# Seven products instead of eight in the first mix and the values, with VectorE's work handed out differently

## The chip, the cores and the metric

The kernel runs on one core of a Trainium2 chip. The metric is the device time in microseconds of one execution. Before the change the median of three runs is 464.14 us (464.13 to 464.68). All data is float32.

## The reference, cut to what matters

The input X has 4 batches of 1024 tokens with 256 features. Four blocks follow each other, and each adds its result to x:

```python
x = x + attn(layernorm(x))      # causal attention, one head of 256
x = x + ffn(layernorm(x))       # "first mix"
x = x + state(layernorm(x))     # gated state-space block
x = x + ffn(layernorm(x))       # "second mix", the same weights

# attn: Q, K, V = X Wq' + bq, X Wk' + bk, X Wv' + bv
#       out = softmax(causal(Q K' / 16)) V
# ffn:  xr, xk = mixtures of x and x one token earlier (mu_r, mu_k)
#       out = sigmoid(xr W_r') * (relu(xk W_k')^2 W_v')
# state: x_proj, z = split(xn W_in' + b_in); a long convolution over 16 states;
#       out = ((conv W_C' + D x_proj) * silu(z)) W_out' + b_out + xn
```

## The kernel before

A batch of 1024 tokens is two halves of 512; a half is numbered j from 0 to 7, and a tile of 128 tokens i from 0 to 31. A matrix of 256 features lies as two chunks of 128 partitions. Nearly all the work of TensorE is dense float32 products, and each shows in the trace as two records with a weight load each.

The program does not write out the order of the engines' work. Python code describes units of TensorE work (`o.unit`) and operations of the other engines (`o.op`), each with what it needs, an estimated cost and the engines that could do it ("ways"). A planner (`class Order`) plays this through with its own model of time, tries twenty sets of its parameters, and emits the instructions of the plan that ends first. Units come in the order in which the code lists them, and the planner may take any of the next nine (`AHEAD`). An operation with two ways goes to the engine that would end it first. A way written `DVE+port`, and every way of `POOL`, also takes a port that the two share in the planner's model. Sums with memory operands alone can go to VectorE or GpSimd, copies out of PSUM to ScalarE or VectorE.

PSUM is two pairs of banks (`pair`, for scores of up to 1024 columns) and four single banks (`bank`, for everything else). In SBUF, 34 slots of equal size hold all the tiles that come and go.

The stages, in order of time:

- *Attention*, from 15 to 253 us: a loop over the 32 tiles. For each: scores (`scores`, L1550), their minimum and exponents, a transpose by way of DRAM, and the weighted sum with the values (`weigh`, L1655). The queries of a half come from `queries` (batches 0 and 1) or from `queries_of_batch` (2 and 3). Values come tile by tile from `values` (L1522): two products of 257 columns, whose last column is a bias for the scores, and an addition of the bias row on VectorE (L1532).
- *First mix* (`mix1`): from i = 10 on, one half in four tiles is worked on beside the attention: keys (`keys`, two units of two products of 512 columns, then relu and square), gates (`gates`, products of 256 columns, then tanh), values (`values`, then a product with the gate on VectorE, L1095, and an addition to x on GpSimd, L1101). Halves 5, 6 and 7 end behind the loop, up to 278 us. `state_prepare` follows each half's values: layer norm and transpose for the state block.
- *State block*, 278 to 397 us: gates and skips of batch 0 plain, of batches 1 to 3 by seven products, the convolution, and outputs of each half (`outputs(j)`), behind which the second mix of that half is prepared.
- *Second mix* (`mix2`), up to the end: keys of batches 0 to 2 by seven products, all gates and values plain. The layer-norm sums of halves 0 to 5 are done on ScalarE (`BY_SCALAR = 6`), the others by VectorE's statistics.

*Seven products.* Where a 256 by 256 weight matrix meets a batch's 256 by 1024 data, both are seen as two by two blocks, and eight block products of 512 columns can be had with seven. `stream_sums` makes four sums of data blocks (T1 to T4, on GpSimd or VectorE, L832), `weight_sums` four of weight blocks, once. `seven_products` is a chain: product 1 goes into the first half of a PSUM pair (the chain) and is copied out (u1); product 2 has a bank of its own and gives the first result; product 6 is accumulated onto product 1 in place, copied out (u2); product 5 goes to the second half; product 7 onto the chain, copied out (u3); product 4 onto the chain, which is the second result; product 3 onto product 5. Three of the four results are sums of a PSUM part and a copy, made by VectorE (L905, L907). A chain yields after each product, and the caller mixes its steps with other units (`go_on`, `next(chain)`, `more_gates`, `advance`).

Of the kernel before, what the change touches and what calls it, by code (L numbers as in the profile page):

```python
# [19 lines left out]
P = 128  # L20
# [10 lines left out]
SLOT = 4 * (D + 1)  # L31
# [10 lines left out]
BY_SCALAR = 6  # L42
# [11 lines left out]
class Order:  # L54
# [17 lines left out]
    SURE = 0.5  # L72
    FRONT = 12.0
# [182 lines left out]
    def _way(self, time, n):  # L256

        if self.log[n]["moves"]:
            time = max(time, self.queue - self.FLIGHT - 0.5)
        return min(  # L260
            (self._start(time, w) + w[1], self._start(time, w), w[0], w[2])
            for w in self.log[n]["ways"]
        )
# [96 lines left out]
def dve(n):  # L360
    return 0.02 + n / 850
# [7 lines left out]
def hybrid_kernel(  # L369
# [41 lines left out]
    slots = ctx.enter_context(tc.tile_pool(name="slots", bufs=34))  # L411
# [92 lines left out]
    wv = new("wv", KC, D + 1)  # L504
    bv_r = new("bv_r", D + 1)
    bq_c, bk_c, dsk, dt_c = (new(n, KC) for n in ("bq_c", "bk_c", "dsk", "dt_c"))
# [14 lines left out]
    load(2.0, "wv", *stream_rows(wv[:, :, :D], WvT), *per_row(bv_r[:, :D], bv))  # L521
# [62 lines left out]
    def normalized(  # L584
# [36 lines left out]
        def stats(n):  # L621
            nc.vector.bn_stats(st()[:, n, :], row(n))  # L622
            nc.vector.bn_aggr(mv()[:, n, :], st()[:, n, :])
# [77 lines left out]
        else:  # L701
            for n in range(NH):
                o.op(f"{key}.st{n}", [needs[n]], ("DVE", 0.53, partial(stats, n)))
            variances_of, shifts_of = variances, shifts
        for n0, n1 in spans:
            span = "" if n1 - n0 == NH else f"{n0}"
            some = range(n0, n1)
            o.op(
                f"{key}.ve{span}", [f"{key}.st{n}" for n in some],
# [105 lines left out]
    def stream_sums(key, src, needs):  # L815
# [9 lines left out]
        for k, plus, minus in (  # L825
# [5 lines left out]
            def emit(engine, k=k, plus=plus, minus=minus):  # L831
# [4 lines left out]
                ("POOL", 1.05, partial(emit, nc.gpsimd)), ("DVE+port", dve(HALF), partial(emit, nc.vector)),  # L836
# [3 lines left out]
    def seven_products(key, sums_key, a, s_of, src, t_of, add_to, direct, needs, there):  # L840


        u = lazy(lambda: slot(f"u_{key}"))
        held = lazy(lambda: pair(f"held_{key}"))

        def part(k):
            return lambda: u()[:, ts(k, HALF)]

        def chain():
            return held()[:, :HALF]  # L850

        def shared():
            return held()[:, HALF:]

        def unit(r, w, data, need, dst, takes=None, first=True):
            o.unit(
                f"{key}.p{r}", columns(HALF), needs + need,
                lambda: nc.tensor.matmul(  # L858
                    dst(), lhsT=w(), rhs=data(), start=first, stop=True, skip_group_check=True
                ),  # L860
                takes,
            )

        def kept(name, r, k, more=()):
            o.op(f"{key}.{name}", [f"{key}.p{r}", *more], *copies(part(k), chain))

        unit(1, lambda: a(0, 0), lambda: src(0)[:, 0, :], there, chain, "pair")
        kept("u1", 1, 0)
        yield
        p = lazy(lambda: bank(f"p2_{key}"))  # L870
        unit(2, lambda: a(0, 1), lambda: src(0)[:, 1, :], there, p, "bank")
        o.op(
            f"{key}.c11", [f"{key}.p2", f"{key}.u1"],
            ("DVE", dve(HALF) + 0.03, partial(add_to, 0, 0, p, part(0))), frees="bank",
        )
        yield
        unit(6, lambda: s_of(2), lambda: t_of(2), [f"{key}.u1", f"{sums_key}.T2"], chain, first=False)
        kept("u2", 6, 1)
        yield
        unit(5, lambda: s_of(1), lambda: t_of(1), [f"{key}.p1", f"{sums_key}.T1"], shared)  # L880
        yield
        unit(7, lambda: s_of(3), lambda: t_of(3), [f"{key}.u2", f"{sums_key}.T3"], chain, first=False)
        kept("u3", 7, 0, [f"{key}.c11"])
        o.op(
            f"{key}.c22", [f"{key}.p5", f"{key}.u3"],
            ("DVE", dve(HALF) + 0.03, partial(add_to, 1, 1, shared, part(0))),
        )
# [1377 lines left out]
```

## Time and profile before

The profiled execution took 464.18 us; its span from the first to the last instruction is 462.4 us, and the granted clock of TensorE is 1.00 throughout.

| stretch (us) | what it holds | TensorE busy | VectorE busy | ScalarE busy | GpSimd busy |
|---|---|---|---|---|---|
| 0 to 80.9 | loads, first tiles of attention | 79.5 | 62.4 | 28.4 | 11.2 |
| 80.9 to 268 | attention and first mix | 187.1 | 166.1 | 90.2 | 52.1 |
| 268 to 346.8 | end of first mix, convolution, first outputs | 77.9 | 46.7 | 39.6 | 34.0 |
| 346.8 to 416.2 | outputs and second mix | 69.4 | 65.9 | 50.4 | 26.8 |
| 416.2 to 462.4 | end of second mix | 40.6 | 29.4 | 18.4 | 15.4 |

Busy time of TensorE is from the start of a record to its modelled end; records overlap, so a stretch is full when they also start one right behind the other. The chain of waits is followed back from the last instruction; a line of it names the engine and line that the end hung on. In the tables of operations the columns are line, engine, operation, output and inputs, sizes, count, busy us, mean ns of one, and the idle time before them with what ended it.

### The profile page before, as it was taken

What the parts mean: (1) busy time and instruction counts of PE and PEld (TensorE: products, weight loads), DVE (VectorE), ACT (ScalarE), POOL (GpSimd) and SP (SyncE); (2) the same over time, 40 slices, a digit from 0 to 9 for tenths busy, and PEclk for the clock granted to TensorE, in tenths of its full rate; (3) what the DMA queues carried; (4) which work ended last, traced back from release to release, by engine and by line L of the source; (5) the groups of instructions that cost most, each with busy time, mean ns of one, the idle gap of its engine ahead of it and who ended that gap; (6) DMA issues with size and microseconds to landing.
All of it is one profiled execution on the core that took longest, in us unless ns stands there. A gap on an engine that the chain in (4) does not pass through costs nothing.

```text
span 462.4 us, 6630 instructions
## 1 busy us (share of the span) xinstructions
PE 454.6 (98%) x2052; PEld 311.4 (67%) x2052; DVE 370.7 (80%) x914; ACT 227.0 (49%) x473; POOL 139.4 (30%) x145
## 2 busy tenths in 40 slices
PE   8999999999999999999999999999999999999996
PEld 5665776667786767776678774473565857686675
DVE  4898697989989888788989977425689989998852
ACT  3322334453284453554335755523467887743452
POOL 3001002303032412332221568512255216336240
PEclk9999999999999999999999999999999999999999
DMA  8067958684358641428784869503014042604522
GB/s 236 27 170 209 272 143 236 169 252 151 101 160 213 184 138 51 137 87 256 226 261 128 276 220 276 213 15 90 13 63 121 0 143 86 215 14 135 178 75 68
DMA packets 84915, 69.44 MB, mean 150 GB/s; under 512 B 20160, under 2 KB 82576, under 8 KB 84880
## 3 DMA queue, kind: packets, MB, share of 16 engines
q1 hardware_dynamic: 84064, 68.76, 50.2%
q8 instruction: 16, 0.26, 0.2%
q10 hardware_dynamic: 816, 0.26, 0.2%
q14 instruction: 19, 0.16, 0.1%
HBM read 40.54 MB, written 28.45 MB: 149 GB/s over the span
## 4 chain that ended last, share of the span: by engine, by line
PE 84%; DVE 10%; POOL 3%; issue 1%; SPq 1%; DMA 1%; ACT 0%; DVEq 0%; POOLq 0%
PE po L1655 14%; PE sc L1550 13%; PE pv L1522 6%; PE held_zs L858 3%; PE held_ss L858 3%; PE held_qs L858 2%; PE held_gks L858 2%; PE pc L1862 2%; PE dust L1339 1%; DVE T_gks L832 1%; DVE xr_g L977 1%; DVE xk_g L977 1%; POOL x L1101 1%; PE pp_a0.pq L793 1%; PE pp_g6.pk L793 1%
## 5 line engine op out<-in xcount | busy, mean ns | idle before, releaser
L1655 PE MATMUL po<-v,prT 128*128 128x256 f32 x288 | 67.6, 380 | 0.0
L1550 PE MATMUL sc<-xa,q 128*128 128x512 f32 (+3 forms) x192 | 66.9, 486 | 0.0
L1655 PEld LDWEIGHTS po<-v,prT 128*128 128x128 f32 x288 | 54.2, 189 | 11.6 <-issue 3.1
L1571 ACT ACTIVATE pr<-pr,nmx 128x128 f32<-128x128 f32 (+7 forms) x32 | 24.7, 773 | 69.7 <-DVE pr L1566 57.1
L1550 PEld LDWEIGHTS sc<-xa,q 128*128 128x128 f32 x192 | 34.8, 190 | 24.3 <-issue 20.1
L1522 PE MATMUL pv<-wv,xa 128*128 128x257 f32 x128 | 32.7, 380 | 0.0
L1101 POOL TENSOR_TENSOR x<-x,r_f 128x512 f32<-128x512 f32 x16 | 20.8, 1298 | 35.7 <-DVE r_f L1095 33.8
L1522 PEld LDWEIGHTS pv<-wv,xa 128*128 128x128 f32 x128 | 23.9, 191 | 8.4 <-issue 4.1
L1608 DVE STREAM_TRANSPOSE prT<-pblocks 128x384 f32<-128x384 f32 (+7 forms) x30 | 24.0, 798 | 4.8 <-DMA pblocks<-exps 4.8
L661 POOL TENSOR_TENSOR rs_h<-ve_h,minus_half 128x8 f32<-128x8 f32 x8 | 13.2, 1646 | 47.9 <-DVE ve_h L650 47.9
L1566 DVE TENSOR_SCALAR_CACHE_REDUCE pr<-sc,v 128x128 f32<-128x128 f32 (+7 forms) x32 | 26.2, 818 | 1.1
L661 POOL TENSOR_TENSOR rs_a<-ve_a,minus_half 128x4 f32<-128x4 f32 x7 | 7.4, 1060 | 62.8 <-DVE ve_a L648 52.9
L1101 POOL TENSOR_TENSOR x<-x,r_g 128x512 f32<-128x512 f32 x14 | 20.1, 1446 | 16.8 <-DVE r_g L1095 16.8
L1699 POOL TENSOR_TENSOR x<-x,bout_r 128x512 f32<-128x512 f32 x16 | 20.7, 1302 | 13.3 <-ACT x L1692 9.8
L1692 ACT ACTIVATE x<-x,mrs_h,rs 128x256 f32<-128x256 f32 x32 | 17.2, 588 | 6.5 <-DVE rs L1703 6.5
L1965 POOL TENSOR_TENSOR z<-z,skip 128x512 f32<-128x512 f32 x11 | 15.0, 1384 | 17.4 <-DVE skip L1961 17.3
L661 POOL TENSOR_TENSOR rs_f<-ve_f,minus_half 128x4 f32<-128x4 f32 x8 | 8.1, 1016 | 39.2 <-DVE ve_f L648 34.1
L1664 DVE SCALAR_TENSOR_TENSOR x<-po,rsm,x 128x256 f32<-128x256 f32 x32 | 14.9, 467 | 5.4 <-PE po L1655 5.3
L622 DVE BATCH_NORM_STATS2 st_a<-x 128x6 f32<-128x256 f32 x32 | 13.0, 407 | 3.0 <-DMA x<-in_L_attn_a_X_dram 3.0
L974 ACT ACTIVATE xk_g<-hT_g,muk 128x512 f32<-128x512 f32 x16 | 11.0, 713 | 8.4 <-DVE hT_g L750 8.4
L1532 DVE TENSOR_TENSOR v<-pv,bv_r 128x257 f32<-128x257 f32 x32 | 13.2, 413 | 2.2 <-PE pv L1522 1.8
L977 DVE SCALAR_TENSOR_TENSOR xr_g<-hT_g,mur,xr_g 128x512 f32<-128x512 f32 x16 | 14.4, 920 | 0.5 <-ACT xr_g L974 0.5
(478 smaller groups left out, 1070.3 us busy)
## 6 DMA issues: line engine op xcount, KB each, us to landing
hk<-r_dram SPq DMA_DIRECT2D x16, 512.0 KB, 6.6
rows_g<-xn_g SPq DMA_DIRECT2D x8, 512.0 KB, 3.0
blocks_g<-rows_g SPq DMA_DIRECT2D x32, 128.0 KB, 2.7
x<-in_L_attn_a_X_dram SPq DMA_DIRECT2D x7, 512.0 KB, 5.1
rows_f<-xn_f SPq DMA_DIRECT2D x7, 512.0 KB, 3.5
blocks_f<-rows_f SPq DMA_DIRECT2D x28, 128.0 KB, 2.7
rows_h<-xn_h SPq DMA_DIRECT2D x7, 512.0 KB, 3.3
blocks_h<-rows_h SPq DMA_DIRECT2D x28, 128.0 KB, 2.9
```

What stands on the lines that cost most here:

```text
L661: nc.gpsimd.tensor_tensor(rs()[:, :k].rearrange("p k n -> p (k n)"), ve()[:, :k].rearrange("p k n -> p (k n)"), minus_half[:, : k * NH], A ...
L858: lambda: nc.tensor.matmul(dst(), lhsT=w(), rhs=data(), start=first, stop=True, skip_group_check=True),
L977: nc.vector.scalar_tensor_tensor(t()[:, c, :], hT()[:, c, :HALF], mu1[:, c : c + 1], t()[:, c, :], ALU.mult, ALU.add,)
L1101: nc.gpsimd.tensor_add(xg, xg, r()[:, ts(g, 2), :])
L1522: nc.tensor.matmul(pv()[:, : D + 1], lhsT=xaj()[:, c, ts(n, P)], rhs=wv[:, c, :], start=(c == 0), stop=(c == KC - 1),)
L1550: nc.tensor.matmul(sc()[:, k * HALF : k * HALF + w], lhsT=qh()[:, c, ts(n, P)], rhs=keys[k]()[:, c, :w], start=(c == 0), stop=(c == KC - 1),)
L1566: nc.vector.tensor_scalar(dst, src, v[2 * b + h]()[:, n, D : D + 1], None, ALU.add, ALU.min, accum_out=nmx(),)
L1571: nc.scalar.activation(p()[:, :nk], p()[:, :nk], AF.Exp, bias=nmx(), scale=-1.0, accum_out=sm())
L1608: nc.vector.transpose(dst()[:, : NH * width].rearrange("p (k m a) -> p k m a", m=NH, a=GRP), blocks().rearrange("p m (k a) -> p k m a", a= ...
L1655: nc.tensor.matmul(po()[:, :D], lhsT=src()[:, ts(n, P)], rhs=v[2 * b + n // NH]()[:, n % NH, :D], start=(n == 0), stop=(n == t),)
L1692: nc.scalar.activation(xt, xt, AF.Identity, bias=mrs()[:, 0, n : n + 1], scale=rs1()[:, n : n + 1])
L1699: nc.gpsimd.tensor_add(xg, xg, bout_r.unsqueeze(1).to_broadcast([P, 2, D]))
```

## The change

- Keys and gates of batches 0 to 2 in the first mix are made by seven products per batch (`keys_of_batch`, and a new `gates_of_batch` with products of 128 columns, the data block as the weights). The two chains are stepped in turn (`mixed`), from the sixth tile of the next batch on.
- Values of batches 2 and 3 of the attention are made by seven products per half of the tiles (`values_of_batch`, products of 129 columns), stepped in turn with the queries' chain (`attended`), whose data sums they share. The row of values has 258 columns, a zero column first.
- These chains, the queries' too, take two single banks instead of a pair.
- The bias of the values is no longer added to the values but to x, by GpSimd (`shifted`, in `attend_prepare`); the values leave PSUM by a copy. The column for the scores still gets its bias, by GpSimd, one tile at a time (`whole_bias`).
- The planner counts 0.5 us more for a way of VectorE where there is another (`SPARED`), after 24 us. Stream sums and the gated product on GpSimd are estimated at 1.25 us instead of 1.05. The aggregations of layer-norm statistics become one operation behind the four statistics.
- Second mix: `BY_SCALAR` is 3 instead of 6. Slots: 33 instead of 34.
- Values and state preparation of halves 4 and 5 stand behind the loop, after keys and gates of half 6. In the last phase the state gates, outputs and keys are listed in another order.

```diff
-BY_SCALAR = 6
+BY_SCALAR = 3
...
+    SPARED = 0.5
...
+        for engine, cost, emit in ways:
+            start = self._start(time, (engine, cost, emit))
+            late = start + cost
+            if len(ways) > 1 and engine[:3] == "DVE" and time > 2 * self.FRONT:
+                late += self.SPARED
+            if late < best:
+                best, chosen = late, (start + cost, start, engine, emit)
...
-    slots = ctx.enter_context(tc.tile_pool(name="slots", bufs=34))
+    slots = ctx.enter_context(tc.tile_pool(name="slots", bufs=33))
...
+    def row_products(tiles, width, *of):
+
+        def emit(dst, w, data, first):
+            for n, t in enumerate(tiles):
+                nc.tensor.matmul(
+                    dst()[:, ts(n, width)], lhsT=data()[:, ts(t, P)], rhs=w(),
+                    start=first and n == 0, stop=True, skip_group_check=True,
+                )
+
+        return len(tiles) * width, columns(width, len(tiles)), operands(*of), emit
...
         u = lazy(lambda: slot(f"u_{key}"))
-        held = lazy(lambda: pair(f"held_{key}"))
+        if kind == "pair":
+            held = lazy(lambda: pair(f"held_{key}"))
+            chain, shared = lambda: held()[:, :n], lambda: held()[:, HALF : HALF + n]
+        else:
+            banks = [lazy(lambda k=k: bank(f"held{k}_{key}")) for k in range(2)]
+            chain, shared = lambda: banks[0]()[:, :n], lambda: banks[1]()[:, :n]
...
+        def gates_of_batch(self, b, kind):
...
+            def add_to(e, h, p, u):
+                nc.vector.tensor_add(out(e, h), by_tile(p), by_tile(u))
...
+            T = stream_sums(key, src, there)
...
+        def shifted(g):
+            xg = x[b][:, h * NH + 2 * g : h * NH + 2 * g + 2, :]
+            nc.gpsimd.tensor_add(xg, xg, bv_r[:, :D].unsqueeze(1).to_broadcast([P, 2, D]))
...
-            ("DVE", dve(D), lambda: nc.vector.tensor_add(t()[:, n, :], pv()[:, : D + 1], bv_r)),
-            frees="bank",
+            *copies(lambda: t()[:, n, :], lambda: pv()[:, :VW], VW), frees="bank",
...
+            ("POOL", 0.15, lambda: nc.gpsimd.tensor_add(
+                t()[:, n, D + 1 :], t()[:, n, D + 1 :], bv_r[:, D:])),
...
+    def values_of_batch(b, T):
...
+        for g in range(2):
...
+            yield from seven_products(
+                key, f"qs{b}",
+                row_products(
+                    range(2 * g, 2 * g + 2), VW // 2, wv_block, lambda k: v_sums[:, k - 1, :], src, T
+                ),
+                add_to, direct, ["v_sums"], there, kind="bank",
+            )
...
+    def mixed(b):
+
+        keys, gates = mix1.keys_of_batch(b, "bank"), mix1.gates_of_batch(b, "bank")
+        for _ in range(7):
+            next(keys)
+            yield
+            next(gates)
+            yield
...
+    def attended(b):
+
+        queries = queries_of_batch(b)
+        next(queries)
+        yield
+        values = values_of_batch(b, query_sums[b])
+        for _ in range(6):
+            next(queries)
+            yield
+            next(values)
+            yield
+        for _ in values:
+            yield
...
+        if i % NT == 0 and SEVEN_FROM <= i // NT + 1 < NB:
+            chain = chain_of(partial(iter, chain), partial(attended, i // NT + 1))
+        if i % NT == 5 and 13 <= i:
+            chain = chain_of(partial(iter, chain), partial(mixed, i // NT - 1))
...
-    both(mix1.values, 5)
-    state_prepare(5)
-    more_gates(0)
-    mix1.keys(6, 0)
+    for unit in (
+        partial(mix1.keys, 6, 0), partial(mix1.keys, 6, 1),
+        partial(mix1.gates, 6, 0), partial(mix1.gates, 6, 1),
+    ):
+        next(chain, None)
+        next(chain, None)
+        unit()
+    for _ in chain:
+        pass
     mix1.transpose(7)
-    mix1.keys(6, 1)
-    both(mix1.gates, 6)
-    more_gates(0)
+    for j in (4, 5):
+        both(mix1.values, j)
+        state_prepare(j)
...
-    more_gates(5)
+    more_gates(2)
     mix_states(1)
+    more_gates(2)
     outputs(1)
-    more_gates(4)
+    more_gates(1)
     outputs(2)
-    more_gates(4)
+    more_gates(2)
+    outputs(3)
+    more_gates(2)
     mix_states(2)
```

## The prediction

> **What bounds the kernel now.** I read the page's busy shares and its chain first, then the table by stage, then the chain in order of time and the waits of TensorE, and last the rows of single operations.
>
> ```profile
> PE 454.6 (98%) x2052; PEld 311.4 (67%) x2052; DVE 370.7 (80%) x914; ACT 227.0 (49%) x473; POOL 139.4 (30%) x145
> ...
> PE 84%; DVE 10%; POOL 3%; issue 1%; SPq 1%; DMA 1%; ACT 0%; DVEq 0%; POOLq 0%
> ```
>
> A busy PE need not be a PE at its peak, so the starts of single products have to show it. The timeline at 110 us does:
>
> ```profile
> 108.67 2.33 PE L1655 MATMUL po<-v,prT 128*128 128x256 f32 x10
> 110.84 0.61 PE L1550 MATMUL sc<-xa,q 128*128 128x128 f32 x4
> 111.28 1.03 PE L1522 MATMUL pv<-wv,xa 128*128 128x257 f32 x4
> ```
>
> Ten records of 256 columns take 2.17 us to the next group's start, 0.217 each, and four of 128 columns take 0.44, 0.111 each (0.108 would be half of the 256). The pieces of the chain agree:
>
> ```profile
> 69.21 3.43 PE pp_a3.pq L793 x8
> ...
> 72.64 0.87 PE pv L1522 x4
> ...
> 89.02 1.73 PE pr_f0.pr L928 x8
> ```
>
> Eight records of 512 columns are 3.43 us, so one product (two records) is 0.858. Products stand back to back like this through the attention. What TensorE waits for in the whole span is little:
>
> ```profile
> PE pr_g4.pv L928 <- ACT ka_g L1047: 0.9, 1, 0.9
> PE held_gks L858 <- DVE u_gks L784: 0.9, 1, 0.9
> PE held_zs L858 <- DVE z L907: 0.6, 1, 0.6
> ```
>
> So each product left out is time won, as long as the other engines keep up. Who is near its limit is read by stage (columns: PE, PEld, DVE, ACT, POOL busy):
>
> ```profile
> 80.90:268.00 187.10, 187.10 (x807) 135.30 (x806) 166.14 (x444) 90.24 (x170) 52.08 (x51) 1.00 0.61 177
> 268.00:346.80 78.80, 77.92 (x504) 44.14 (x503) 46.73 (x93) 39.56 (x89) 33.99 (x31) 1.00 0.38 120
> 346.80:416.20 69.40, 69.40 (x278) 49.68 (x277) 65.94 (x112) 50.43 (x126) 26.76 (x27) 1.00 0.31 96
> ```
>
> The granted clock is 1.00. In the loop of attention and first mix (80.9 to 268) VectorE is 89% busy and TensorE never starves. From 346.8 to 416.2 VectorE is 95% busy and TensorE still runs full, so 95% is the most that this trace shows VectorE carrying without a loss.
>
> **TensorE, part by part.** *Keys* (three batches): eight products of 512 columns become seven; 3 x 0.858 = 2.6 us less. *Gates* (three batches): now 32 products of 256 columns per batch, four row pieces of 1.73 = 6.92 us. Then 7 x 4 products of 128 columns, each with its own weight load: 56 records at 0.111 = 6.22. Gain 0.7 each, 2.1 in all. *Values* (two batches): now eight tiles of 0.87 = 6.96. Then 2 x 7 x 2 products of 129 columns, 56 records at 0.111 = 6.22; gain 0.74 each, 1.5 in all. The sixteen tiles left alone grow from 257 to 258 columns, under 0.1. Sum: **6.1 us less on TensorE**, at 0.108 a record 6.7.
>
> Each seven-product run is a chain: product 6 waits for a copy out of PSUM, 7 and 4 for the next copies. Eleven such chains run today (two of queries, three each of gates, skips and second-mix keys), and the waits above charge two of them with 0.9 and 0.6: 0.14 a chain. The change adds ten (three keys, three gates, four values): **1.4 us back**. Ends: nothing, if other units always fill in, and 0.9 each, 9 us in all, if none does (first rival below).
>
> **VectorE.** Rows used:
>
> ```profile
> L1532 DVE TENSOR_TENSOR v<-pv,bv_r 128x257 f32<-128x257 f32 x32 | 13.2, 413 | 2.2 <-PE pv L1522 1.8
> ...
> L905 DVE TENSOR_TENSOR ka_g<-held_gks,u_gks 128x512 f32<-128x512 f32 x6 | 4.0, 674 | 1.4 <-ACT ka_g L1046 1.3
> L1038 DVE SCALAR_TENSOR_TENSOR ka_g<-ka_g 128x512 f32<-128x512 f32 x6 | 4.1, 676 | 0.1
> L1699 POOL TENSOR_TENSOR x<-x,bout_r 128x512 f32<-128x512 f32 x16 | 20.7, 1302 | 13.3 <-ACT x L1692 9.8
> L832 DVE TENSOR_TENSOR T_qs<-xa,T_qs 128x512 f32<-128x512 f32 x3 | 3.1, 1042 | 0.0
> ```
>
> Gone: 32 bias additions to v (13.2; the copies in their place fit on ScalarE) and three relus of 0.67 (2.0). New: 18 sums of 512 columns for keys and gates at 0.674 (12.1), 12 value sums at 0.413 (5.0), nine squarings at 0.676 (6.1; ScalarE could take them at 1.25), eight small weight sums at most 0.287 (the 128-column mask addition), 2.3. Net +10.3 with nothing moved. The half-microsecond handicap on VectorE moves work that has a second way: in the loop 16 normalized rows (8.5), six stream sums (5.2), seven more rows (2.7), two copies (1.4): up to 17.8. Net between -7.5 and +10.3; I take 0, most of two thirds moved, since ScalarE (90 of 187 us) has room for rows at 0.59 and six copies and two tanh in the new form.
>
> GpSimd takes 24 stream sums at 1.27 (30.5), sixteen bias additions to x at 1.30 (20.8) and 32 one-column additions at some 0.2 (a two-column copy took 0.19): about 58 us more, most of it in the loop, where it has 52. It is then at most 60% busy, but it works against VectorE: the stream sum on VectorE is 0.68 in its quiet form and 1.04 in the form of the row above, and the mixing sums xk_f and xr_f mean 0.81 and 0.77 in the loop against 0.68. That excess, 14 x 0.13 + 14 x 0.09 = 3.1 us, came with 52 us of GpSimd; twice the GpSimd adds 3 us to VectorE.
> The Trainium skill (SBUF — State Buffer, section "SBUF: two separate sides") says the port pair of the two engines is locked for a whole instruction and the other fully blocks. Estimated by that rule, 45 more GpSimd operations of 1.29 us, each meeting a two-input VectorE operation with chance 0.3 (some 45 of these in 187 us) and holding it for half its length, would cost 8.5 us, which speaks against the change.
> I keep the 3 of the rows.
>
> So VectorE has 166 + 0 + 3 = 169 of 181 us, 93%: under the 95% seen, and I charge nothing. If it gets +10.3 + 3 it has 179.5, which at 95% needs 189 us, 1.9 more than now.
>
> **Queues.** The transposes by DRAM of halves 4 to 7 are asked for four steps earlier, and values of halves 4 and 5 of the mix move behind the loop, with their state preparation (1 write, 4 reads each on SP) past two sets of keys and gates. SP issues the same transfers; DMA is 61% busy in the loop. The bias addition to x stands before the attention's own addition; GpSimd runs it tens of microseconds ahead of need, and late it would hold that addition's bank, then the next value product. The earlier halves hold their slots some 30 us longer (four tiles of the 32 that take 15 to 253 us), and there is one slot fewer (33): that costs nothing unless a T or u tile must wait for a slot; no row shows a slot wait, so 0 to 2 us, I take 0.
>
> **Last phase.** Statistics of three halves go back from ScalarE to VectorE: 12 x (0.41 + 0.18) = 7.1 us more, against up to 4.7 (rows), 5 (sums) and 4 (squarings) that the handicap moves away. The small aggregations of the statistics (0.18 each) are gathered behind the four statistics, as many as before. The finer order spreads state gates between outputs. Waits to be won there are the three above, 2.4 us; at the other end VectorE at 95% gives as much again. I take 0.5 won.
>
> **Sum.** -6.1 + 1.4 - 0.5 = -5.2. The profiled execution took 464.18 us (span 462.4 and 1.8 around it), as good as the median of 464.14: **459.0 us**. No change can be told within 0.2%, 0.9 us.
>
> **Rivals.** *Banks.* Two interleaved chains hold four single banks, all that there are, from the second one's fifth product to the first one's fourth. Until then no po, pv or gate product can start, only scores. Against: scores have their own pairs again, which queries took before. Seven such pairings, up to 2 x 0.65 of copies each, cost at most 9 us; half, 4.6, gives 464.18 - 6.6 + 4.6 = 462.2. Chance 0.17, ending between 461 and 465.
>
> *Slower: VectorE or the port becomes the bound in the loop.* Point: above 187.1 x 0.95 = 177.7 us of VectorE work, 11.6 more than now, the loop is longer than today. +10.3 and 3 for the port gives 189 in the loop and, other things equal, 466; with the 28 mixing sums each 0.36 longer, as the T_qs row is, the port costs 10.1 instead of 3.1 now, 7 more: 183.4 at 95% is 193, 470. For it: 18 new PSUM sums cannot leave VectorE, slices of today's loop stand at 11.37 of 11.58. Against: the 17.8 us that can move. Chance 0.22.
>
> *Pile-up behind the loop.* Four state preparations instead of three lie close: from values 4 to values 7 TensorE has 5 x 3.45 = 17.3 us, GpSimd needs 4 x (2 x 1.27 + 1.65 + 2 x 1.29) = 27. Urgent of it is 17, so it just fits; if the last half's statistics queue behind two additions of x, TensorE idles 2.6 to 5 us: 461.6 to 464. Chance 0.1.
>
> **Chances and range.** Forecast 0.51 (456 to 461.5, faster). Of banks, 0.10 is faster, 0.05 no change, 0.02 slower; of the pile-up, 0.05 is faster and 0.05 no change; VectorE's 0.22 is slower. Faster 0.66, same 0.10, slower 0.24. The range runs from 455.5 (0.108 a record, no chain waits, 2.4 won late: 464.2 - 6.7 - 2.4 = 455.1, rounded in) to 467.5, leaving out the dear end of VectorE.
>
> **What would show it.** Right: PE busy about 6 us less in all, gates and value products 0.111 apart, the loop under 183 us with TensorE still at 100% in it; VectorE's busy time within 5 us of 371, GpSimd's near 195. Wrong: rows of PE waiting for u_fks, u_frs, u_vs copies or VectorE sums above 0.2 us a chain; VectorE over 95% across the loop; a gap of TensorE before the last half's transposes (h7).

## The result and the profile after

The change takes **467.82 us** (median of 6 runs, 466.16 to 468.73) beside 464.55 us of the kernel before on the same chip (6 runs, 464.13 to 465.43): ratio of the means 1.0065, between 1.0044 and 1.0085 at 95%. It is slower by 0.65%, where 1.1% faster was forecast, and 467.82 lies just above the range's end of 467.5. The profiled execution took 467.66 us, with a span of 465.7.

The first page of the change, busy shares and the engines' shares of the chain of waits:

```profile
PE 451.5 (97%) x2166; PEld 311.9 (67%) x2166; DVE 361.1 (78%) x902; ACT 257.7 (55%) x517; POOL 190.7 (41%) x210
...
PE 69%; DVE 13%; DMA 6%; ACT 5%; SPq 2%; issue 2%; POOL 2%; DVEq 0%; ACTq 0%; POOLq 0%
```

VectorE has 10 us less to do than before, GpSimd 51 more, ScalarE 31 more. TensorE was 84% of the chain and is 69%: for 31% of the span the end now hangs on the others, DMA and SyncE's queue among them. The first place to look would be the new products, but the timeline of TensorE shows them as short as computed:

```profile
104.54 0.61 PE L884 MATMUL p_vs<-wv,xa 128*128 128x129 f32 x4
104.98 1.06 PE L884 MATMUL held_vs<-v_sums,T_qs 128*128 128x129 f32 x8
105.88 0.38 PE L1717 MATMUL sc<-xa,q 128*128 128x256 f32 x1
...
113.43 1.05 PE L884 MATMUL held_frs<-w_r,xr_f 128*128 128x128 f32 x8
114.32 1.02 PE L874 MATMUL p_fks<-xk_f,w_fk 128*128 128x512 f32 x2
```

Four records of the values take 0.44 us from start to start and eight of the gates 0.89: 0.11 each. The second place is VectorE. The table by stretch (PE, PEld, DVE, ACT, POOL busy, then the granted clock):

```profile
80.90:264.50 183.60, 182.87 (x924) 135.88 (x924) 159.19 (x422) 107.25 (x207) 73.21 (x82) 1.00 0.62 177
264.50:346.80 82.30, 80.31 (x519) 47.05 (x518) 52.42 (x116) 49.56 (x115) 43.64 (x38) 1.00 0.44 126
346.80:416.20 69.40, 66.35 (x252) 45.54 (x251) 59.55 (x112) 42.64 (x79) 25.27 (x23) 0.98 0.30 93
416.20:465.70 49.50, 43.39 (x171) 30.99 (x169) 32.14 (x63) 21.31 (x37) 18.58 (x16) 1.00 0.32 106
```

VectorE is 87% busy in the loop and 86% from 346.8 on, less than before in both. No engine is full where TensorE isn't. What differs is in the column of TensorE: from 264.5 to 416.2 it is less full than before (98 and 96%; before, the stretches from 268 and 346.8 had 99 and 100), and the last stretch, 88% full in both, is 3.3 us longer. So I measured its *stops*: a stop is where a record starts later than the columns of the record before it take (0.217 us for 256 columns), counted above 0.09 us (a regular gap of 0.10 to 0.11 us and the short gaps among the convolution's small products left out). A time given for a stop is the start of the record before it. Most of the time lost to half clock falls into it too.

| stops of TensorE, us | before | change |
|---|---|---|
| first 15 us | 2.7 | 3.3 |
| attention and first mix | 0.2 | 1.9 |
| to the end of the convolution's products | 0.4 | 2.4 |
| to the outputs of half 3 | 1.0 | 0.2 |
| outputs of halves 4 to 7 | 0.1 | 5.4 |
| the rest | 2.1 | 3.0 |
| sum | 6.5 | 16.2 |
| span without stops | 455.9 | 449.5 |

That is the whole result in two lines: **6.4 us of TensorE's work won, 9.7 us of stops added**; 3.3 us slower. (With every gap above 0.12 us counted and no other, it is 5.9 and 9.2.)

Who ends the longest stops is in the waits (what waits, for what; total, times, longest):

```profile
PE held_zs L874 <- ACT u_zs L802: 2.3, 1, 2.3
PE held_zs L874 <- DVE z L953: 2.0, 1, 2.0
...
PE pr_g4.pv L974 <- ACT ka_g L1100: 0.9, 1, 0.9
PE held_ss L874 <- ACT u_ss L802: 0.8, 1, 0.8
...
PE po L1822 <- DVE x L1831: 0.6, 1, 0.6
...
PE po L1822 <- DVE ka_f L951: 0.2, 1, 0.2
```

`held_zs` is a seven-product chain of the state block, one of those that were there before. Neither operation it waits for is slow; both are late. The two lines of `po` belong to the loop: by the code, `po` takes no data from these two sums, and what it waits for is the single bank that each of them empties. For the first long stop (290.8 us) the timeline of the change reads:

```profile
288.12 1.30 DVE L769 STREAM_TRANSPOSE xnT<-blocks_h 128x512 f32<-128x512 f32 x2 [1.27 <-DMA blocks_h<-rows_h]
289.63 1.65 POOL L673 TENSOR_TENSOR rs_h<-ve_h,minus_half 128x8 f32<-128x8 f32 x1 [1.66 <-DVE ve_h L662]
291.24 1.26 POOL L1866 TENSOR_TENSOR x<-x,bout_r 128x512 f32<-128x512 f32 x1
291.31 1.29 DVE L682 SCALAR_TENSOR_TENSOR mrs_h<-rs_h,mv_h 128x4 f32<-128x4 f32 x2 [1.11 <-POOL rs_h L673]
292.52 0.74 DVE L953 SCALAR_TENSOR_TENSOR z<-held_zs,b_all,u_zs 128x512 f32<-128x512 f32 x1
...
293.40 1.10 PE L874 MATMUL held_zs<-T_zs,w_in 128*128 128x512 f32 x2 [1.99 <-DVE z L953]
```

VectorE's queue is in fixed order, so the chain's sum (z, 0.74 us) stands behind all of this: a transpose that waits 1.27 us for a transfer, GpSimd's power of the variance behind it, and two 128x4 products that take 1.29 us in place of some 0.3, since GpSimd's addition (291.24) holds the one that stands beside it. For the second (349.4 us), SyncE's queue, then the rest:

```profile
339.60 0.40 SPq L757 DMA_DIRECT2D rows_g<-xn_g  x1
340.04 3.58 SPq L2065 DMA_DIRECT2D xmT<-m_dram  x4
343.73 1.94 SPq L763 DMA_DIRECT2D blocks_g<-rows_g  x4
...
348.39 1.31 DVE L769 STREAM_TRANSPOSE hT_g<-blocks_g 128x512 f32<-128x512 f32 x2 [1.57 <-DMA blocks_g<-rows_g]
...
349.14 1.33 ACT L1027 ACTIVATE xk_g<-hT_g,muk 128x512 f32<-128x512 f32 x2 [0.70 <-DVE hT_g L769]
350.38 1.32 ACT L1027 ACTIVATE xr_g<-hT_g,mur 128x512 f32<-128x512 f32 x2
351.61 0.56 ACT L802 COPY u_zs<-held_zs 128x512 f32<-128x512 f32 x1
352.22 1.45 PE L874 MATMUL held_zs<-T_zs,w_in 128*128 128x512 f32 x2 [2.28 <-ACT u_zs L802]
```

SyncE issues the four loads of `xmT` in 3.58 us; the planner counts 1.9 (`("SP", 1.9, emit)`). The reads of the transposed rows stand behind them, the transposes behind those, four scalings on ScalarE behind the transposes, and the copy that the chain waits for (0.56 us) behind the scalings. One late transfer passes through three queues before it stops TensorE. In the trace of the kernel before, SyncE's queue has no load of `xmT` between 325 and 362 us.

### The profile page after: what moved, and what is told of

It reads as the page before. It is cut to its first block, busy times and chain, and to the rows that moved or that the text cites. A ratio compares the mean times of both kernels' runs of the same rounds, so it can differ in the third digit from the quotient of the medians.

```text
span 465.7 us, 6996 instructions
## 1 busy us (share of the span) xinstructions
PE 451.5 (97%) x2166; PEld 311.9 (67%) x2166; DVE 361.1 (78%) x902; ACT 257.7 (55%) x517; POOL 190.7 (41%) x210
## 4 chain that ended last, share of the span: by engine, by line
PE 69%; DVE 13%; DMA 6%; ACT 5%; SPq 2%; issue 2%; POOL 2%; DVEq 0%; ACTq 0%; POOLq 0%
PE sc L1717 10%; PE po L1822 9%; PE held_ss L874 3%; PE held_frs L884 3%; PE held_fks L874 3%; PE held_gks L874 3%; PE held_zs L874 2%; PE pv L1634 2%; DMA blocks_g<-rows_g 2%; DMA exps<-pr 2%; PE pc L2029 2%; PE held_qs L874 1%; PE pr_g0.pr L974 1%; SPq L763 1%; DVE prT L1775 1%
## 5 line engine op out<-in xcount | busy, mean ns | idle before, releaser
L1201 POOL TENSOR_TENSOR x<-x,r_g 128x512 f32<-128x512 f32 x14 | 20.8, 1494 | 11.0 <-DVE r_g L1195 11.0
L1653 POOL TENSOR_TENSOR v<-v,bv_r 128x1 f32<-128x1 f32 x32 | 6.3, 207 | 39.5 <-ACT v L802 35.6
L1548 POOL TENSOR_TENSOR x<-x,bv_r 128x512 f32<-128x512 f32 x16 | 20.2, 1272 | 2.3 <-ACT xn_a L694 2.3
L694 ACT ACTIVATE xn_a<-x,mrs_a,rs_a 128x256 f32<-128x256 f32 x24 | 13.1, 592 | 7.1 <-DVE mrs_a L682 7.1
L673 POOL TENSOR_TENSOR rs_f<-ve_f,minus_half 128x4 f32<-128x4 f32 x8 | 8.9, 1112 | 19.7 <-DVE ve_f L660 19.5
L1859 ACT ACTIVATE x<-x,mrs_h,rs 128x256 f32<-128x256 f32 x32 | 16.6, 595 | 0.0
L1634 PE MATMUL pv<-wv,xa 128*128 128x258 f32 x64 | 16.2, 381 | 0.0
L694 ACT ACTIVATE xn_g<-x,mrs_g,rs_g 128x256 f32<-128x256 f32 x24 | 12.9, 592 | 5.8 <-DVE mrs_g L682 4.6
L673 POOL TENSOR_TENSOR rs_a<-ve_a,minus_half 128x4 f32<-128x4 f32 x7 | 7.2, 1032 | 20.5 <-DVE ve_a L660 14.7
L1634 PEld LDWEIGHTS pv<-wv,xa 128*128 128x128 f32 x64 | 12.0, 191 | 4.8 <-issue 2.9
```

The costliest lines, as they stand in the source:

```text
L673: nc.gpsimd.tensor_tensor(rs()[:, :k].rearrange("p k n -> p (k n)"), ve()[:, :k].rearrange("p k n -> p (k n)"), minus_half[:, : k * NH], A ...
L694: nc.scalar.activation(place(n), split(row(n)), AF.Identity, bias=mrs()[:, k - 1, n : n + 1], scale=rs()[:, k - 1, n : n + 1],)
L1201: nc.gpsimd.tensor_add(xg, xg, r()[:, ts(g, 2), :])
L1548: nc.gpsimd.tensor_add(xg, xg, bv_r[:, :D].unsqueeze(1).to_broadcast([P, 2, D]))
L1634: nc.tensor.matmul(pv()[:, :VW], lhsT=xaj()[:, c, ts(n, P)], rhs=wv[:, c, :], start=(c == 0), stop=(c == KC - 1),)
```

## The experiments

All runs in one table. "Plan" says what the kernel is planned from; the ratio is to the kernel before on the same chip; stops, and span without stops, are of the profiled execution, which is one of several: those of one kernel lie 1 to 4 us apart.

| kernel | median us | ratio of the means [95%] | stops | span without |
|---|---|---|---|---|
| before | 464.6 | 1 | 6.5 | 455.9 |
| the change | 467.8 | 1.0065 [1.0044, 1.0085] | 16.2 | 449.5 |
| e1 change, last phase as before | 467.5 | 1.0049 [1.0030, 1.0067] | 15.9 | 450.1 |
| e2 before, new last phase | 468.7 | 1.0082 [1.0063, 1.0102] | 9.2 | 457.6 |
| e3 change, no handicap | 467.1 | 1.0046 [1.0029, 1.0062] | 14.1 | 450.3 |
| e4 change, issue cost | 465.3 | 1.0008 [0.9995, 1.0021] | 14.7 | 450.2 |
| e5 change, values 4 and 5 first | 465.7 | 1.0016 [1.0001, 1.0030] | 11.6 | 450.5 |
| e6 change, second plan | 465.7 | 1.0026 [1.0006, 1.0046] | 12.6 | 450.8 |
| e7 before, second plan | 468.7 | 1.0068 [1.0046, 1.0090] | 11.3 | 455.7 |
| e8 change, no bias on GpSimd | 467.3 | 1.0035 [1.0015, 1.0055] | 16.4 | 449.2 |
| e9 change, third plan | 472.3 | 1.0156 [1.0131, 1.0182] | 19.7 | 450.4 |
| e10 before, third plan | 467.2 | 1.0047 [1.0028, 1.0067] | 9.8 | 456.5 |
| e11 change, longer flight | 463.4 | 0.9966 [0.9950, 0.9982] | 10.6 | 450.7 |
| e12 change, longer lag | 461.8 | 0.9939 [0.9921, 0.9956] | 10.9 | 450.2 |
| e13 before, longer lag | 467.0 | 1.0047 [1.0029, 1.0065] | 10.2 | 455.6 |
| e14 before, lag and issue | 465.7 | 1.0019 [1.0010, 1.0028] | 7.9 | 456.2 |
| e15 change, lag and issue | 464.3 | 0.9992 [0.9974, 1.0010] | 13.2 | 450.2 |
| e16 change, longer lag alone | 462.5 | 0.9950 [0.9932, 0.9967] | 8.5 | 452.1 |
| e17 change, values by eight | 461.8 | 0.9936 [0.9915, 0.9956] | 8.1 | 451.9 |
| e18 change, still longer lag | 464.5 | 0.9996 [0.9986, 1.0005] | 12.1 | 449.7 |

**The last phase (e1, e2).** e1 is the change with the old order of the last phase and `BY_SCALAR = 6`; e2 is the kernel before with the new order and 3.

```diff
-BY_SCALAR = 6
+BY_SCALAR = 3
...
-    more_gates(5)
+    more_gates(2)
     mix_states(1)
+    more_gates(2)
     outputs(1)
```

> The change with the last phase taken back (old order of state gates, outputs and keys, and statistics of six halves on ScalarE again); seven products, values, handicap and single banks stay. Theory A, the new order of the last phase costs the time (stops of TensorE of 2.4 us at 349 us, 1.6 us of half clock behind it, 0.9 at 368, 0.9 at 419, against 2.1 in that stage before): 461 to 462.5 us, faster than before by 2 to 3.5. Theory B, the plan is brittle everywhere once VectorE's work is handed to ScalarE and GpSimd, whatever the order: 465 to 468 us, with stops of about 4 us and more after 346 us in other places.

> The kernel before with nothing but the new last phase (the new order and statistics of three halves on ScalarE instead of six); no new seven products, no handicap. Theory A, the new order costs by itself: 467 to 469 us. Theory B, it needs the handicap to do harm: 463.5 to 465.5 us.

Undone in the change, the new order gives back nothing that can be told (467.5 against 467.8): the stops in the outputs of halves 4 to 7 fall from 5.4 to 1.8 us, those of the loop grow from 1.9 to 5.1, and a new one of 2.0 comes before the convolution, at 305 us. Put alone into the kernel before, it costs 0.8%. So the new order is dear by itself, but it isn't the cause of the loss, which stays without it in other places, some of them long before the part that was altered. Up to there the code of e1 is that of the change, so what reaches back is the planner: another list gives another plan from end to end.

**The handicap of VectorE (e3).**

```diff
-    SPARED = 0.5
+    SPARED = 0.0
```

> The change with the handicap on VectorE at 0 instead of 0.5 us. Theory C, the handicap puts copies out of PSUM (u_zs, u_ss, u_gks) on ScalarE behind additions that wait for late transposes, and TensorE stops for them: 462.5 to 465 us, the copies back on VectorE in part, stops of TensorE for u copies under 1.5 us in all instead of 3.5. Theory A or B without C: 466.5 to 469 us. If the handicap is what keeps VectorE below its bound, as the forecast had it: 468 us and more, VectorE above 93% in the loop.

VectorE does 386 us of work in place of 361, and the time is no worse (467.1). VectorE's total is not what costs.

**The issues' price (e4).**

```diff
-        o.op(f"xmT{b}", ["m"], ("SP", 1.9, emit), moves=[move(4 * S * L, 512)] * 4)
+        o.op(f"xmT{b}", ["m"], ("SP", 3.6, emit), moves=[move(4 * S * L, 512)] * 4)
```

> The change with one number of the planner's model changed: the four loads of xmT of a batch are planned with 3.6 us on the queue of SyncE, as the trace shows them, instead of 1.9. Theory D, the plan is late because this queue takes twice as long as planned, so reads of the second mix's blocks come late behind them: 464 to 466 us and no stop of over 1 us for u_zs between 346 and 358 us. Without D: 467 to 469 us, the stop at about 350 us still there.

465.3 us, 0.6% under the change. The loads move 15 us earlier, the stop near 350 us falls from 2.43 to 0.83 us, but 1.1 us appear at 356, 1.9 at 381 and 2.5 at 80 and 103. The stops are only 1.5 us less where the median fell by 2.5; the profiled execution is one of the longer ones of this kernel (span 464.9).

**The order behind the loop (e5).** Values and state preparation of halves 4 and 5 before keys and gates of half 6.

```diff
-    for unit in (
-        partial(mix1.keys, 6, 0), partial(mix1.keys, 6, 1),
-        partial(mix1.gates, 6, 0), partial(mix1.gates, 6, 1),
-    ):
-        next(chain, None)
-        next(chain, None)
-        unit()
     for _ in chain:
         pass
-    mix1.transpose(7)
     for j in (4, 5):
         both(mix1.values, j)
         state_prepare(j)
+    mix1.transpose(7)
+    both(mix1.keys, 6)
+    both(mix1.gates, 6)
```

> The change with one part of the order behind the loop undone: values and state preparation of halves 4 and 5 stand before keys and gates of half 6 again. Theory P (pile-up), four state preparations so close make the reads of h blocks take 6.0 us instead of 2.9 and stop TensorE for 2.15 us before the last half's transposes: that stop is gone, reads of h blocks back near 3 to 4 us, 465 to 466.3 us. Without P, or if another plan brings its own stops: 467 to 468.5 us.

465.7 us. The stop at 290.8 us is gone, and the blocks of the halves land in 3.3 us in place of 6.0. A stop of 2.2 us comes up at 300 us, before the convolution's products.

**Other plans of the same work (e6, e7, e9, e10).** The planner keeps the plan that ends first in its own model. Here it takes the second (`[1]`) and the third (`[2]`).

```diff
-                if end < best:
-                    best, chosen = end, (plan, used)
+                if end < lowest.get(plan, (math.inf,))[0]:
+                    lowest[plan] = end, used
...
+        end, plan = sorted((end, plan) for plan, (end, _) in lowest.items())[1]
```

> The change, every line of the work as it is, but the planner takes its second best set of parameters (0.3 us later by its own model). It shows how far two plans of the same work lie apart. Theory S (scatter of plans): 464.5 to 471 us, over 1 us away from the change's 467.8, with the stops of TensorE in other places but again 13 to 17 us in sum. If the parts of the change themselves fix the loss: 467 to 468.5 us, the stops where they were.

> The kernel before with its second best set of parameters. Theory S: 464 to 468 us, slower than its own best by up to 3 us, since the kernel before was chosen with this very plan. If the work before is easier to plan than the work after: 464 to 465.5 us, stops of TensorE 6 to 8 us in sum as before.

> The change with the planner's third best set of parameters (0.3 us behind its best by the planner's model). Theory S (two plans of the same work lie microseconds apart, and the plan of the kernel before is a lucky one): the plans of the change so far are 467.8 and 465.7, this one 464.5 to 469 us; with 12 to 16 us of stops.

> The kernel before with its third best set of parameters. Theory S: 465.5 to 470 us, like its second (468.7), above its own best (464.7); then the work before, planned by another hand, is slower than the work after. If the second plan was an exception: 464 to 465.5 us.

The order of the units and their work stay as they are, and the time moves by 4 us for the kernel before (464.6, 468.7, 467.2) and by 6.6 for the change (467.8, 465.7, 472.3). The plan that the kernel before runs is the best of its three; the change has a better second. A difference of 3 us between the two kernels is therefore no more than a plan can do. The scatter is wider than expected: e7 and e9 lie above the ranges of theory S (468 and 469), and e9 has 19.7 us of stops instead of at most 16. The third plan of the change shows that new chains can be hit as well as old ones; its waits:

```profile
PE held_vs L885 <- DVE v L1683: 3.9, 2, 3.2
PE held_qs L875 <- DVE v L1683: 1.5, 1, 1.5
```

The 3.2 us are a chain's own reply: product 3 of the values waits for the sum that empties its bank, and on VectorE that sum stands behind four sums of weights. The queries' chain takes no data from `v`; its 1.5 us are a wait for a bank.

**The shared port (e8).** Same plan as the change, but the sixteen additions of the values' bias to x aren't issued (the output lacks that bias).

```diff
-            nc.gpsimd.tensor_add(xg, xg, bv_r[:, :D].unsqueeze(1).to_broadcast([P, 2, D]))
+            return
```

> The change in its own plan, every other instruction in its place, but the sixteen additions of the values' bias to x on GpSimd are not issued (this leaves that bias out). Theory L (lock): VectorE is held by GpSimd's operations, 24 us over its quiet times instead of 17 before; these sixteen (20 us) are in the attention, where TensorE stops 1.9 us: VectorE's excess falls by 4 us or more and the time to 465 to 466.5 us. If the stops come from late plans at the loop's end and behind it: 466.8 to 468.2 us.

What the operations of VectorE take over the quiet duration of their form (the median of the form, counted from 10% above it) sums to 16.6 us before, 23.9 in the change and 20.8 here. The port does cost VectorE some 3 us for these 20 us of GpSimd, but the stops stay at 16.4: what these sixteen additions hold up is not what stops TensorE. Other additions stayed, the one at 291.24 us among them.

**More slack in the plan (e11, e12).** Both have e4's price and e5's order. e11 counts 1.8 us of flight for a transfer, e12 counts 0.25 us from the end of an operation to the start of what waits for it.

```diff
-    FLIGHT, LANDING = 1.2, 0.24
+    FLIGHT, LANDING = 1.8, 0.24
```

```diff
-    LAG = 0.15
+    LAG = 0.25
```

> The change with values of halves 4 and 5 first (as in the fifth run), the queue cost of xmT planned as measured (as in the fourth), and every transfer planned 0.6 us later (1.8 instead of 1.2 us to its start). Theory D (the plan counts transfers too early, and what waits for them heads a queue): 462 to 464 us, faster than the kernel before, since the two parts alone gave 465.3 and 465.7; stops under 10 us. Theory S alone: 464.5 to 468 us, no better than those two.

> As the run before, but in place of the transfers every operation is planned to be ready 0.1 us later for those that need it (0.25 us instead of 0.15). If it is slack in general that the plan lacks, not transfers: 462 to 464 us. If it is transfers: 464.5 to 467 us. Theory S alone: 464.5 to 468 us.

463.4 and 461.8 us: both beat both kernels, with all the work of the change in them. That still leaves open whether the kernel before would win as much with the same slack.

**The control (e13 to e16).** The lag alone, and the lag with the issues' price, for both kernels.

> The kernel before, with 0.25 instead of 0.15 us planned from the end of one operation to the start of what waits for it. Theory P (the seven products give their 5 to 6 us, the slack only sets it free): the kernel before has few stops to lose (6.5 us of TensorE), so it gains at most 2 us: 462.5 to 466. Theory Q (the gain of the longer planned lag has nothing to do with the products): it falls as far as the change did with it, 3 us or more, to 461.5 or below.

> The kernel before with both: a planned lag of 0.25 us, and 3.6 instead of 1.9 us planned for the four issues of xmT. P: 462.5 to 466, at least 1.5 us above the change with the same two constants (e15). Q: within 1 us of it.

> The change with both constants and nothing else (the order of the mix's tail as in the change). P: between 460.5 and 464.5, stops of TensorE 9 to 13 us instead of 16.2. If the order of the tail was what the best kernel (461.8) owed its time to, it stays at 465 to 466.

> The change with the planned lag of 0.25 us alone, the issues of xmT planned at 1.9 as before. P: the gain comes from slack in general: 462 to 465.5. If the wrong price of the issues is the larger part, the stop near 350 us stays at 2 us or more, and the time at 465 or above.

The kernel before wins nothing from it: 467.0 and 465.7 us, the first even above the 466 that P allowed. Theory Q, which asked for 461.5 or below in e13, falls. The change takes 462.5 with the lag alone, 4.5 us less than the kernel before with the same lag, and 464.3 with both, 1.4 less, just short of the 1.5 that P asked for. P holds in its direction: from neither of these two slacks did the kernel before get what the change got. Busy shares and chain of the change with the longer lag alone:

```profile
PE 451.7 (98%) x2166; PEld 312.5 (68%) x2166; DVE 358.5 (78%) x898; ACT 260.8 (57%) x524; POOL 184.3 (40%) x207
...
PE 93%; DVE 3%; DMA 1%; ACT 1%; issue 1%; SPq 0%; DVEq 0%; ACTq 0%
```

Nearly the same busy times as the change and 5 us less: 93% of the chain is TensorE's, not 69%. The reading that the wrong price of the issues is behind the stops falls here too: with the issues still priced at 1.9 us there is no stop near 350 us (e16), and with the true price there is one of 2.43 us (e15), where `xr_g` comes late on VectorE. The wrong price made one stop of one plan; it is not the reason for them.

**Fewer chains, still more slack (e17, e18).** e17 makes all values tile by tile again, those of batches 2 and 3 too (the two that the change altered; the expectation calls them the first two), all else as in the change; e18 is e12 with a lag of 0.35.

```diff
-        values = values_of_batch(b, query_sums[b])
-        for _ in range(6):
-            next(queries)
-            yield
-            next(values)
-            yield
-        for _ in values:
+        for _ in queries:
             yield
...
-            if valued < 2 * NH * SEVEN_FROM:
-                values(valued)
+            values(valued)
```

> The change with the first two batches' values by eight tiles again, as all others; keys and gates by seven products stay. TensorE has 1.5 us more to do (455.9 - 4.6 = 451.3 us of work without stops). Theory R (more products by seven mean more replies of other engines to wait for, so the stops shrink with the number of chains, four of ten gone): stops of 12 us or less, 463 to 466. Theory S (the stops come from how a plan happens to fall, not from the number of chains): stops anywhere between 8 and 20 us, time at 461 to 473, TensorE's work without stops up by 1.5 us all the same.

> The order of the mix's tail of e5, 3.6 us for the issues of xmT, and a planned lag of 0.35 instead of the 0.25 of e12. If more slack in the plan steadily gives fewer stops: stops below 10 us and 459.5 to 462. If 461.8 was one fall of the plan among others: 462 to 467.

e17 takes 461.8 us with the planner's constants as they were. Without stops its span is 451.9 us (451.3 expected), and the stops are 8.1, the fewest of any kernel with the new products. Its page:

```profile
PE 451.3 (98%) x2118; PEld 311.6 (68%) x2118; DVE 354.3 (77%) x904; ACT 251.3 (55%) x503; POOL 195.2 (42%) x212
...
PE 97%; DVE 2%; ACT 1%; issue 0%; DVEq 0%; ACTq 0%
```

That fits theory R in its stops (the time lies under R's 463), fewer chains, fewer stops; but e16 reaches 8.5 with all the chains, so one plan doesn't exclude S. e18 says that slack helps by falls of the plan and not steadily: 0.35 gives 464.5 and 12.1 us of stops, worse than 0.25.

**What the runs settle.** The work of the change can be faster than the kernel before: e12 and e17, 461.8 us, 0.6% under it. These are the best of thirteen kernels with new chains (e8 left out), against six without. Set side by side with equal planning (as handed over, second plan, third plan, lag, lag and price), the change stands to the kernel before at +0.65, -0.4, +1.1, -1.0 and -0.3%, from the ratios in the table. In the profiled executions of these ten, the span without stops is 456.0 us on average before and 450.6 with the change: 5.4 us won, in every pair (3.5 to 6.4). The stops average 9.1 and 14.0 us: 4.9 lost, in four pairs of five (-1.7 to 9.9). So the products give most of their computed gain each time, and on the average over these plans the added stops take nearly all of it. The 0.65% that was measured is one fall of that.

The place of the added stops differs between the pair as handed over and the average. In that pair 7.4 of the 9.7 us are behind the loop. Over the five pairs (gaps above 0.12 us) the stops behind the loop average 5.3 us before and 5.7 with the change, and those in the loop, up to 264.5 us, 0.2 and 4.0. No kernel without the new chains has more than 0.6 us there; of the thirteen with them only e11, e12 and e17, which has four chains fewer, have less than 1.6. Of the 4.0 us, 1.8 stand directly before a product of a new chain. So the change's plans do have more stops where the new chains are, though e11 and e12 (0.2 and 0.1 us) show that a plan with all ten can avoid them. What remains open is by which way: more replies awaited from other engines (44 more operations of ScalarE and 65 more of GpSimd in fixed order), the single banks, or both. e17 speaks for the number of chains, and no run shows one of these alone.

## Why the prediction was wrong

- **TensorE, 6.1 us less: right.** 6.4 us in this pair, 5.4 over five, at 0.11 us a record as read off the score products. (At 0.108 us a record the sum would have been 7.0, not 6.7.)
- **Chains, 1.4 us back: near in this pair by luck.** The loop, which holds all ten new chains, has 1.7 us more stops, but none above 0.12 us stands before a product of a new chain; over the five pairs it has 3.8 us more. The long waits of this pair are in chains that were there before.
- **VectorE, net 0: pessimistic.** In the loop it fell by 6.9 us (166.1 to 159.2), near the favourable end of -7.5, and in the whole span by 9.6. That it would not be the bound in the loop was right: 87%.
- **The port, 3 us in the loop: half of it came, with less than half of the GpSimd work.** There GpSimd grew by 21 us (52.1 to 73.2) and not by most of 58, and VectorE's excess over quiet durations by 1.5 (5.7 to 7.2); the row I scaled (3.1 us beside 52 of GpSimd) would give 1.3 for 21. The 8.5 us by the rule of the Trainium skill (SBUF — State Buffer, "SBUF: two separate sides") were for 45 more operations of GpSimd; by the same working 21 us of them give 3.1, an estimate, twice what came. Over the whole span the excess rose by 7.3 us (16.6 to 23.9) with 51 us more of GpSimd, most of it outside the loop. The row that I scaled (28 mixing sums) missed the small operations: 128x4 products held for a microsecond. At 87% busy neither figure would have been the loss by itself, and e8 shows that 3 us given back don't change the stops.
- **Queues at nothing, and 0.5 us won in the last phase: the step that failed.** By these two terms the time behind the loop should not have grown; its stops grew by 7.4 us (3.6 to 11.0), and e1 shows that most of the loss stays when the last phase is taken back. "SP issues the same transfers; DMA is 61% busy in the loop" charged the moved work at nothing. The count of transfers was right, the order wasn't looked at: the page gives the median from issue to landing of a half's blocks as 6.0 us, 2.9 before, and the first long stop begins with one of these. The second begins with reads of other blocks (`blocks_g`, median 2.6 us, 2.7 before), which are not slow but are issued late, behind the loads of `xmT`. The two stops and the half clock behind the second are some 6 of the 11.0 us. Without them (e4, e5) other stops come up, so they are the form that the loss took in this plan. The two lines, before and after:

```profile
blocks_h<-rows_h SPq DMA_DIRECT2D x28, 128.0 KB, 2.9
```

```profile
blocks_h<-rows_h SPq DMA_DIRECT2D x28, 128.0 KB, 6.0
```

- **Under both, the rule that misled: "each product left out is time won, as long as the other engines keep up", with keeping up read from busy shares.** "Under the 95% seen, and I charge nothing" is true of shares and says nothing of moments. An engine at 60 to 87% whose queue is in fixed order can still hand one operation over 2 us late, and TensorE, also in fixed order, stands. In all the sum charged 0.9 us for waiting (1.4, 0 and -0.5), and 9.7 were added. The kernel before stops for 6.5 us where its other plans stop for 8 to 11; I took that for a property of the work, and it was one of the plan.
- **Last phase, 0.5 us won: wrong in sign.** Alone it costs 0.8% (e2), 3.8 us. "The finer order spreads state gates between outputs" looked at the spacing of TensorE's units and not at which reply each of them waits for.
- **The rivals.** The pile-up behind the loop named the right place and nearly the price (a stop at 290.8 us of 2.15, at 2.6 to 5 predicted) and the right make, GpSimd's additions in front of VectorE's small operations. It was one of ten waits above 0.3 us. "VectorE becomes the bound" gave 466 to 470, which holds the time, by a mechanism that the profile refutes. Banks: right in kind at a small size, `po` waiting 0.6 and 0.2 us for a bank in the loop, where 4.6 was the price; in e9 the queries' chain waits 1.5. The case that came, many short waits all over with no engine full, was in none of them.

## What to carry to other kernels

Where instructions are laid out in fixed queues by a planner, the time of a change is work on the bottleneck plus stops, and the two must be told apart: the starts of the bottleneck's records give both. Here the work saved came nearly as computed; the stops moved with the plan, and the three plans of the same work lay up to 4 us apart before the change and 6.6 with it, about as much as the change's worth. So measure two or three plans of each version before judging either, ask of each moved operation which queue it stands in and what stands behind it, and don't read from an average busy share that a neighbour answers in time.

## What the hardware showed unasked

A 128x4 operation of VectorE took 1.2 us in place of 0.15 where a GpSimd addition ran beside it (L682 for `mrs_h`: least 0.119, median 0.154, most 1.212 us). In proportion a small operation loses most: eightfold here, where the 512-column sum `T_qs` of the prediction went from 0.68 to 1.04 us.

After the stop at 349 us, TensorE ran at half clock. Stretches of 2 and 3 us of the change (the granted clock is the third number from the end):

```profile
349.00:352.00 3.00, 0.95 (x2) 0.12 (x2) 3.00 (x7) 2.86 (x5) 0.84 (x2) 1.00 0.40 113
352.00:354.00 2.00, 1.78 (x3) 0.65 (x4) 2.00 (x2) 1.95 (x8) 1.05 (x1) 0.72 0.44 96
354.00:356.00 2.00, 2.00 (x6) 1.55 (x6) 2.00 (x5) 0.89 (x3) 0.46 (x1) 0.50 0.00 0
356.00:358.00 2.00, 2.00 (x10) 1.76 (x9) 1.85 (x4) 1.02 (x2) 1.19 (x1) 0.92 0.00 0
```

Taken together that is some 3.4 us at half (0.28 x 2 x 2, plus 2, plus 0.08 x 2 x 2). Sixteen records of 256 columns took 4.85 us to the next start, where 3.47 is their time: a stop of 2.4 us cost 1.4 more behind it. The same happened after stops of 2.43 (e15) and 1.69 us (e13), but not after 2.15 (290.8 us) or 1.63 (e17). In e2 it happened near 352 us, and in e10 near 398, with no stop above 0.6 us. In these five cases the products of 16 rows (`py`) had just run, but so they had in e17. In e12 it happened at 427 us, after a stop of 1.57, without them, and the longest stop of all, 3.35 us (e9, 112 us), was not followed by it. The Trainium skill (TensorE: Matmul & The Clock Gate, "HAM oscillation — how this bites in real kernels") warns of idle gaps above some 3.4 us; the length of the half-clock stretch agrees with its window of 3.4 us, but here shorter gaps were enough and a gap of 3.35 us was not always enough. What sets it off was not tried.

An issue of an `xmT` load cost SyncE 0.9 us (3.58 for four; 2.83 in e16), one of `rows_g` 0.4 and of `blocks_g` 0.43 to 0.49.
